# Gate products of a GRU by seven block products instead of eight, on one NeuronCore

## The chip, the cores and the metric

The kernel runs on one core of one Trainium2 chip. The metric is the device time of one execution in microseconds, taken on the slowest core, which here is the only one. Engines are named as in the profile: PE is the matrix engine (PEld its weight loads), DVE the vector engine, ACT the scalar engine, POOL the GpSimd engine, SP the queue that issues transfers.

## The reference

The input is 128 graphs of 128 nodes with 256 features, all float32, and an integer adjacency matrix for each graph. Four layers follow each other, and after each the result is added to its input and normalised over the features:

```python
# layer 0, three steps with shared GRU weights
for i in range(3):
    m = h @ weight[i]
    aggr = A.T @ m                       # A = (adj != 0)
    gi = aggr @ w_ih.T + b_ih ; gh = h @ w_hh.T + b_hh
    r = sigmoid(i_r + h_r) ; z = sigmoid(i_z + h_z) ; n = tanh(i_n + r * h_n)
    h = (1 - z) * n + z * h
x = layernorm(x + h)
# layers 1 to 3, each with its own W and a
Wh = x @ W.T ; e = leaky(Wh @ a1 [:, None] + Wh @ a2 [None, :]) masked by adj
x = layernorm(x + softmax(e) @ Wh)
```

## The kernel before

The 128 graphs are worked on in 32 groups of four (`G = 4`), so that a group's nodes fill 512 columns (`GN`). Features lie on partitions in two chunks of 128 (`KC = 2`). The function `gru` records layer 0 of a group, `gat` records layers 1 to 3 of it. Nothing is issued while they record: each operation goes to a `Plan` with the engines that may run it, a price in nanoseconds for each, the tiles it reads and writes, and the group's number as its priority. `Plan.order` then walks through time with these prices, gives every engine that is free the ready operation of the lowest group number for which slots are free, and returns one list. The engines' instruction streams follow that list, and each engine works its own stream strictly in order. So the order is fixed before the kernel runs, by the written prices.

Before the groups, three weight products `wc` (the message weight folded into the input weight, L488) and the score vectors `wa` (L496) are made.

A GRU step of a group goes like this. L317 multiplies the transposed state by the adjacency matrix into a `bank` tile of PSUM, and it is copied out as `agg` (L253 on ACT or L255 on DVE). The gates are the products of L328, in `gate` tiles of PSUM: for each of the two output chunks `c`, the accumulators `phn` (2 products with the state `hT`), `pr` (2 with `hT`, 2 with `agg`), `pin` (2 with `agg`) and `pz` (4), each product a 128x128 weight block against 512 columns. That is 24 products in a step and 2304 in the kernel. Then L343 (ACT, `q`), L347 (ACT, `tr`), L351 and L354 (DVE, `q` and `s`), L356 (ACT, `n`), L359 (ACT, `tz`), L362 (POOL, `d = hT - n`), L364 and L366 (DVE, `d` and the new `hT`) follow. L378 transposes the new state back for the next step.

A graph-attention layer begins when the layer norm of the one before (L278 and L280 on DVE, L282 and L284 on POOL, L287 on DVE) has given `xn`. Eight DVE operations at L400 (`fx`) form two scores for each of the four graphs, L409 on PE spreads them, L414 to L425 on DVE, L418 and L429 on ACT make the softmax, L436 transposes it, L452 and L463 on PE apply it and the weights (L463 has 128x256 products), and L469 on DVE scales and adds. While one group is in `gat`, the next is in `gru`; the list interleaves them.

## Time and profile before

| What | Value |
|---|---|
| median of 3 runs (lowest, highest) | 2953.62 us (2953.50, 2954.26) |
| the profiled execution, its time and its span | 2953.93 us, 2952.1 us |
| PE busy, matmul records | 2900.2 us, 11080 |
| DVE, ACT, POOL busy | 1729.7, 1079.8, 432.7 us |
| mean granted PE clock | 0.992 |
| one group in the steady part (2769.98 to 2859.55) | 89.57 us: PE 89.41, DVE 52.67, ACT 33.49, POOL 13.46 |

The profile counts two records for one float32 product (2304 products of L328 stand as two groups of 2304 records), so a product's price is that of two records. A record's mean duration includes the way through the array, which overlaps the next record; what a product costs PE is the distance between starts, and that is read from the timeline.

### The profile page before, as it was taken

Reading aid. Unit: us, or ns where it says so; the run is one execution under the profiler, and the core shown is the slowest. Engines: PE = TensorE matmul, PEld = TensorE weight load, DVE = VectorE, ACT = ScalarE, POOL = GpSimd, SP = SyncE. Lnnn points to the kernel's source line nnn. Section 1 sums busy time; section 2 is a strip of 40 time slices with the busy share of each in tenths; the row PEclk is TensorE's granted clock in tenths of the full one; section 3 lists DMA queues with packets and bytes.
Section 4 is the critical chain, followed back from the end, with each engine's and each line's share of the span. In section 5 each row is a group of like instructions: output and inputs, shape, how many; then the busy total and the mean of one; then the engine's idle time right before and its main releaser. Section 6 shows DMA issues by size and latency. Waiting matters only on the chain.

```text
span 2952.1 us, 31887 instructions
## 1 busy us (share of the span) xinstructions
PE 2900.2 (98%) x11080; PEld 1713.8 (58%) x11080; DVE 1729.7 (59%) x5639; ACT 1079.8 (37%) x2446; POOL 432.7 (15%) x454
## 2 busy tenths in 40 slices
PE   8999999999999999999999999999999999999994
PEld 4555565555555556555555655555655565565553
DVE  2566565556665655665665655566656556656654
ACT  2333333333343333333333334333433333333331
POOL 0111111111111111111111111111111111111110
PEclk9999999999999999999999999999999999999996
DMA  2000000000000000000000000000000000000000
GB/s 89 11 18 18 11 8 18 18 18 18 12 8 18 18 19 11 18 8 19 18 18 11 8 18 18 18 19 11 8 18 19 19 11 18 8 15 8 8 8 8
DMA packets 52001, 47.93 MB, mean 16 GB/s; under 512 B 2048, under 2 KB 51200, under 8 KB 51840
## 3 DMA queue, kind: packets, MB, share of 16 engines
q1 hardware_dynamic: 50688, 41.95, 4.5%
q10 hardware_dynamic: 1152, 3.94, 0.4%
q8 instruction: 87, 1.43, 0.2%
q14 instruction: 74, 0.61, 0.1%
HBM read 29.11 MB, written 16.78 MB: 16 GB/s over the span
## 4 chain that ended last, share of the span: by engine, by line
PE 88%; DVE 9%; POOL 2%; issue 0%; DMA 0%; ACT 0%; POOLq 0%; ACTq 0%; DVEq 0%
PE gate L328 59%; PE bank L463 9%; PE bank L452 6%; PE bank L317 6%; PE bank L378 3%; DVE fx L400 3%; DVE y L469 2%; POOL rstd L284 2%; DVE xn L287 2%; PE bank L436 2%; DVE st L278 2%; PE bank L409 1%; PE bank L268 1%; DVE mv L280 1%; POOL ve L282 1%; PE gate L488 1%
## 5 line engine op out<-in xcount | busy, mean ns | idle before, releaser
L328 PE MATMUL gate<-hT,whh 128*128 128x512 f32 x2304 | 1082.8, 593 | 0.0
L328 PE MATMUL gate<-agg,wc 128*128 128x512 f32 x2304 | 1072.0, 592 | 0.0
L328 PEld LDWEIGHTS gate<-agg,wc 128*128 128x128 f32 x2304 | 423.3, 190 | 447.7 <-issue 446.1
L328 PEld LDWEIGHTS gate<-hT,whh 128*128 128x128 f32 x2304 | 415.0, 191 | 387.0 <-issue 378.0
L362 POOL TENSOR_TENSOR d<-hT,n 128x512 f32<-128x512 f32 x192 | 243.9, 1271 | 1667.4 <-ACT n L356 1667.4
L463 PE MATMUL bank<-gwT,aT 128*128 128x256 f32 x1536 | 350.5, 381 | 0.0
L463 PEld LDWEIGHTS bank<-gwT,aT 128*128 128x128 f32 x1536 | 293.4, 191 | 81.0 <-issue 37.1
L359 ACT ACTIVATE tz<-gate,brz 128x512 f32<-128x512 f32 x192 | 130.8, 681 | 457.5 <-PE gate L328 457.5
L469 DVE SCALAR_TENSOR_TENSOR y<-bank,rden,xn 128x256 f32<-128x256 f32 x384 | 164.9, 471 | 199.0 <-PE bank L463 199.0
L400 DVE SCALAR_TENSOR_TENSOR fx<-xn,wa 128x256 f32<-128x256 f32 x768 | 272.5, 419 | 0.0
L351 DVE SCALAR_TENSOR_TENSOR q<-tr,q 128x512 f32<-128x512 f32 x192 | 132.1, 688 | 231.3 <-ACT tr L347 231.3
L347 ACT ACTIVATE tr<-gate,brz 128x512 f32<-128x512 f32 x192 | 131.9, 687 | 366.1 <-PE gate L328 366.1
L287 DVE TENSOR_SCALAR xn<-y,mv,rstd 128x256 f32<-128x256 f32 x512 | 176.8, 409 | 143.3 <-POOL rstd L284 143.3
L356 ACT ACTIVATE n<-s,bin__95 128x512 f32<-128x512 f32 x192 | 138.1, 719 | 329.6 <-DVE s L354 329.6
L452 PEld LDWEIGHTS bank<-pT,xn 128*128 128x128 f32 x1536 | 191.2, 196 | 47.4 <-issue 37.1
L364 DVE SCALAR_TENSOR_TENSOR d<-tz,d 128x512 f32<-128x512 f32 x192 | 131.9, 687 | 136.2 <-ACT tz L359 117.7
L278 DVE BATCH_NORM_STATS2 st<-y 128x6 f32<-128x256 f32 x512 | 207.3, 405 | 1.1
L418 ACT ACTIVATE e<-e,f 128x128 f32<-128x128 f32 x384 | 125.6, 390 | 211.2 <-DVE top L414 211.2
L452 PE MATMUL bank<-pT,xn 128*128 128x128 f32 x1536 | 192.5, 280 | 2.0 <-ACT pT L253 2.0
L354 DVE TENSOR_TENSOR s<-gate,q 128x512 f32<-128x512 f32 x192 | 132.4, 690 | 85.3 <-PE gate L328 75.4
L253 ACT COPY agg<-bank 128x512 f32<-128x512 f32 x161 | 94.2, 585 | 215.2 <-PE bank L317 215.2
L343 ACT ACTIVATE q<-gate,bhn 128x512 f32<-128x512 f32 x192 | 130.9, 682 | 113.6 <-PE gate L328 113.6
(55 smaller groups left out, 2239.0 us busy)
## 6 DMA issues: line engine op xcount, KB each, us to landing
xs<-in_x_dram SPq DMA_DIRECT2D x32, 512.0 KB, 3.9
out_dram<-xn SPq DMA_DIRECT2D x32, 512.0 KB, 2.9
adj<-in_adj_dram SPq DMA_DIRECT2D x32, 256.0 KB, 2.8
wih<-in_w_ihT_dram ACTq DMA_DIRECT2D x1, 768.0 KB, 5.3
gw<-in_gnn_wT_dram ACTq DMA_DIRECT2D x1, 768.0 KB, 7.8
whh<-in_w_hhT_dram ACTq DMA_DIRECT2D x1, 768.0 KB, 9.5
gwT<-in_gat_wT_dram ACTq DMA_DIRECT2D x1, 768.0 KB, 5.1
gatw<-in_gat_w_dram ACTq DMA_DIRECT2D x1, 768.0 KB, 6.3
```

The source lines that it names most:

```text
L278: plan.op({"DVE": 350}, lambda e, b=b, st=st: nc.vector.bn_stats(T(st), T(y)[:, b, :]), reads=[(y, b)], writes=[st], prio=prio)
L287: plan.op({"DVE": 345}, lambda e, b=b: nc.vector.tensor_scalar(T(dst)[:, b, :], T(y)[:, b, :], T(mv)[:, b, 0:1], T(rstd)[:, b:b + 1], op0= ...
L317: nc.tensor.matmul(T(b_)[:, b * P:(b + 1) * P], src, T(am)[:, b, :], start=True, stop=True)
L328: plan.op({"PE": 860}, lambda e, w=w, m=m, k=k, j=j: nc.tensor.matmul(T(dst), w(k), T(m), start=(j == 0), stop=(j == len(todo) - 1)), read ...
L351: plan.op({"DVE": 720}, lambda e, q=q, tr=tr: nc.vector.scalar_tensor_tensor(T(q), T(tr), 1.0, T(q), op0=ALU.add, op1=ALU.mult), reads=[tr ...
L354: plan.op({"DVE": 720}, lambda e, s=s, q=q, pin=pin: nc.vector.tensor_add(T(s), T(pin), T(q)), reads=[pin, q], writes=[s], prio=prio)
L356: plan.op({"ACT": 640}, lambda e, n=n, s=s, c=c: nc.scalar.activation(T(n), T(s), AF.Tanh, bias=bin_[:, c:c + 1]), reads=[s], writes=[n], ...
L362: plan.op({"POOL": 1266}, lambda e, d=d, n=n, c=c, hT=hT: nc.gpsimd.tensor_tensor(T(d), T(hT[c]), T(n), ALU.subtract), reads=[hT[c], n], w ...
L400: plan.op({"DVE": 345}, lambda e, b=b, h=h, l=l, f=f, fx=fx, xc=xc: nc.vector.scalar_tensor_tensor(T(fx), T(xc)[:, b, :], 1.0, wa[:, l, h, ...
L452: nc.tensor.matmul(T(b_)[:, b * P:(b + 1) * P], T(xc)[:, b, c * P:(c + 1) * P], T(pT)[:, b, :], start=True, stop=True)
L463: nc.tensor.matmul(T(b_)[:, (b - b0) * D:(b - b0 + 1) * D], T(aT[k])[:, b * P:(b + 1) * P], gwT[:, l, k, :], start=(k == 0), stop=(k == KC ...
L469: nc.vector.scalar_tensor_tensor(T(y)[:, b, :], T(b_)[:, (b - b0) * D:(b - b0 + 1) * D], T(rden)[:, b:b + 1], T(xc)[:, b, :], op0=ALU.mult ...
```

## The change

The gate products are made by a form of Strassen's algorithm (Winograd's). The 256x256 weight of each gate is taken as 2x2 blocks of 128x128, the 256x512 moving matrix as 2x2 blocks of 128x256, and the four blocks of the output come from seven block products in place of eight. The weights' sums (`block_sums`) are made once, at the beginning. The moving matrices' sums are made in each step, for `hT` and for `agg`, by four POOL subtractions of 128x256 each (`sums`, L374 of the changed program). In `strassen` the two gates r and z go together through three `gate` banks, and the two halves of n likewise; a bank is copied out on ACT (`kept`: L462, or L466 and L469) between products that go on accumulating in it, and DVE adds a kept part to a bank (`add`, L409 of the changed program). A product is now 128x128 by 128x256, 42 in a step (L404 of the changed program).

Beside that, SBUF tiles lose their own pools: there are a few sizes of slots (`k2`, `k4` and others), shared by all that fit, and the plan hands out the slot numbers, keeping some free for the oldest group (`own`). At most four groups may be in `gru` at a time (`gru`, 4). Group 0 makes the weights as part of the plan. The residual `x` is loaded a second time at the end of `gru`, and the mask `no` is made in place of `am`.

```diff
+    pools = {"gru": 4, "xs": 2, "adj": 2, "am": 4, "k2": 26, "k4": 18, "fx": 2, "f": 3, "mv": 4, "st": 6, "v": 16,
+             "gate": 5, "bank": 3}
+    own = {"k2": 8, "k4": 5, "gate": 2, "v": 5}
+    floats = {"gru": 0, "k4": 1024, "xs": 1024, "fx": 256, "f": 8, "mv": 8, "st": 6, "v": 4}
...
-    GATES, BANKS = 5, 3
-    pools = {"xs": 3, "adj": 2, "am": 2, "no": 3, "some": 3, "hT": 6, "agg": 4, "h2": 4, "q": 2, "tr": 2,
-             "s": 2, "n": 2, "tz": 2, "d": 2, "y": 2, "xn": 4, "f": 2, "fx": 2, "aT": 4, "e": 2, "p": 2, "pT": 2,
-             "mv": 4, "st": 4, "ve": 4, "rstd": 4, "top": 4, "nmax": 4, "den": 4, "rden": 4}
-    plan = Plan({**pools, "gate": GATES, "bank": BANKS})
...
+    def block_sums(dst, a, keys, prio):
+
+        d = T(dst)
+        todo = [(A11, lambda e: copy(e, d[:, A11], a(0, 0)), [], EVICT2),
+                (A12, lambda e: copy(e, d[:, A12], a(0, 1)), [], EVICT2),
+                (S1, lambda e: nc.vector.tensor_add(d[:, S1], a(1, 0), a(1, 1)), [], {"DVE": 600}),
+                (S2, lambda e: nc.vector.tensor_sub(d[:, S2], d[:, S1], a(0, 0)), [S1], {"DVE": 600}),
+                (S3, lambda e: nc.vector.tensor_sub(d[:, S3], a(0, 0), a(1, 0)), [], {"DVE": 600}),
+                (S4, lambda e: nc.vector.tensor_sub(d[:, S4], a(0, 1), d[:, S2]), [S2], {"DVE": 600}),
+                (N22, lambda e: nc.scalar.mul(d[:, N22], a(1, 1), -1.0), [], {"ACT": 500})]
+        for m, fn, more, engines in todo:
+            plan.op(engines, fn, reads=keys + [(dst, j) for j in more], writes=[(dst, m)], prio=prio)
...
+    def sums(ms, prio):
+
+        t = Buf("k4", 4, H)
+        first, second = (lambda: T(ms[0])[:, 0:H]), (lambda: T(ms[0])[:, H:GN])
+        third, fourth = (lambda: T(ms[1])[:, 0:H]), (lambda: T(ms[1])[:, H:GN])
+        part = lambda j: lambda: T(t)[:, j, :]
+        for j, (a, b, reads) in enumerate((
+                (second, first, [ms[0]]), (fourth, part(0), [ms[1], (t, 0)]), (fourth, second, ms),
+                (part(1), third, [ms[1], (t, 1)]))):
+            plan.op({"POOL": 700}, lambda e, j=j, a=a, b=b: nc.gpsimd.tensor_tensor(
+                T(t)[:, j, :], a(), b(), ALU.subtract), reads=reads, writes=[(t, j)], prio=prio)
+        return t
+
+    def moving(m, ms):
+
+        half = {A11: (0, 0), A12: (1, 0), S4: (1, 1)}
+        if m in half:
+            c, j = half[m]
+            return ms[0][c], lambda: T(ms[0][c])[:, j * H:(j + 1) * H]
+        j = {S1: 0, S2: 1, S3: 2, N22: 3}[m]
+        return (ms[1], j), lambda: T(ms[1])[:, j, :]
+
+    def strassen(gates, kept, prio):
+
+        bx, by, bz = Buf("gate", GN), Buf("gate", GN), Buf("gate", GN)
+        o0, o1 = Buf("k4", 2, GN), Buf("k4", 2, GN)
+        p1, u2, p5 = Buf("k2", GN), Buf("k2", GN), Buf("k2", GN)
+
+        def product(dst, m, first):
+            todo = [(j, gt, w, ms) for j, (gt, sides) in enumerate(gates) for w, ms in sides]
+            keys = {moving(m, ms)[0]: 0 for _, _, _, ms in todo}
+            keys.update({(w, m): 0 for _, _, w, _ in todo})
+            if first:
+                keys.update({(ms[1], 3): 0 for _, _, _, ms in todo})
+
+            def fn(e):
+                for n, (j, gt, w, ms) in enumerate(todo):
+                    nc.tensor.matmul(T(dst)[:, j * H:(j + 1) * H], T(w)[:, m, gt, :], moving(m, ms)[1](),
+                                     start=first and n == 0, stop=n == len(todo) - 1, skip_group_check=True)
+            plan.op({"PE": 432 * len(todo)}, fn, reads=list(keys), writes=[dst], prio=prio)
+
+        def add(b_, part, o, j):
+            plan.op({"DVE": 720}, lambda e: nc.vector.tensor_add(
+                T(o)[:, :, j * H:(j + 1) * H], T(b_).rearrange("p (g n) -> p g n", g=2),
+                T(part).rearrange("p (g n) -> p g n", g=2)),
+                reads=[b_, (part, 0), (part, 1)], writes=[(o, j)], prio=prio)
+
+        product(bx, A11, True)
+        kept(p1, bx, 0)
+        product(bz, S1, True)
+        kept(p5, bz, 1)
+        product(bx, S2, False)
+        kept(u2, bx, 0)
+        product(bz, S4, False)
+        add(bz, u2, o0, 1)
+        product(bx, S3, False)
+        add(bx, p5, o1, 1)
+        product(by, A12, True)
+        add(by, p1, o0, 0)
+        product(bx, N22, False)
+        return o0, o1, bx
...
-            def gate(dst, terms):
-
-                todo = [(w, m, k) for w, ms in terms for k, m in enumerate(ms)]
-                for j, (w, m, k) in enumerate(todo):
-                    plan.op({"PE": 860}, lambda e, w=w, m=m, k=k, j=j: nc.tensor.matmul(
-                        T(dst), w(k), T(m), start=(j == 0), stop=(j == len(todo) - 1)),
-                        reads=[m], writes=[dst], prio=prio)
-
-            def W(gt, c):
-                return lambda k: whh[:, k, gt * D + c * P:gt * D + (c + 1) * P]
-
-            def C(gt, c):
-                return lambda k, i=i: wc[:, i, k, gt * D + c * P:gt * D + (c + 1) * P]
-
+            h_in, a_in = (whs, (hT, sums(hT, prio))), (wcs[i], (agg, sums(agg, prio)))
+
+            def whole(dst, src, c):
+                plan.op({"ACT": 560}, lambda e: nc.scalar.copy(T(dst), T(src)),
+                        reads=[src], writes=[(dst, 0), (dst, 1)], prio=prio)
+
+            def halves(dst, src, c):
+                plan.op({"ACT": 370}, lambda e: nc.scalar.activation(
+                    T(dst)[:, 0:H], T(src)[:, 0:H], AF.Identity, bias=bhn[:, c:c + 1]),
+                    reads=[src], writes=[(dst, 0)], prio=prio)
+                plan.op({"ACT": 370}, lambda e: nc.scalar.copy(T(dst)[:, H:GN], T(src)[:, H:GN]),
+                        reads=[src], writes=[(dst, 1)], prio=prio)
+
+            rz = strassen([(0, (h_in, a_in)), (1, (h_in, a_in))], whole, prio)
+            nn = strassen([(2, (h_in,)), (2, (a_in,))], halves, prio)
+            hT2 = []
             for c in range(KC):
...
+
+                o, v, d = rz[c], nn[c], Buf("k2", GN)
+
+                def tanh(gt, n0, n1, src, o=o, c=c):
+                    nc.scalar.activation(T(o)[:, gt, n0:n1], src(), AF.Tanh,
+                                         bias=brz[:, gt * KC + c:gt * KC + c + 1], scale=0.5)
+                for gt in range(2):
+                    if c == 0:
+                        plan.op({"ACT": 640}, lambda e, gt=gt, o=o, tanh=tanh: tanh(gt, 0, GN, lambda: T(o)[:, gt, :]),
+                                reads=[(o, 0), (o, 1)], writes=[(o, 2 + gt)], prio=prio)
+                    else:
+                        plan.op({"ACT": 420}, lambda e, gt=gt, tanh=tanh, rz=rz: tanh(
+                            gt, 0, H, lambda: T(rz[2])[:, gt * H:(gt + 1) * H]),
+                            reads=[rz[2]], writes=[(o, 4 + gt)], prio=prio)
+                        plan.op({"ACT": 400}, lambda e, gt=gt, o=o, tanh=tanh: tanh(gt, H, GN, lambda: T(o)[:, gt, H:GN]),
+                                reads=[(o, 1), (o, 4 + gt)], writes=[(o, 2 + gt)], prio=prio)
+                if c == 1:
+                    plan.op({"ACT": 370}, lambda e, v=v, nn=nn: nc.scalar.activation(
+                        T(v)[:, 0, 0:H], T(nn[2])[:, 0:H], AF.Identity, bias=bhn[:, 1:2]),
+                        reads=[nn[2]], writes=[(v, 0)], prio=prio)
+                plan.op({"DVE": 720}, lambda e, o=o, v=v: nc.vector.scalar_tensor_tensor(
+                    T(v)[:, 0, :], T(o)[:, 0, :], 1.0, T(v)[:, 0, :], op0=ALU.add, op1=ALU.mult),
+                    reads=[(o, 2), (v, 0), (v, 1)], writes=[(v, 2)], prio=prio)
+                if c == 0:
+                    plan.op({"DVE": 720}, lambda e, v=v: nc.vector.tensor_add(T(v)[:, 0, :], T(v)[:, 1, :], T(v)[:, 0, :]),
+                            reads=[(v, 2)], writes=[(v, 3)], prio=prio)
+                else:
+                    plan.op({"DVE": 430}, lambda e, v=v, nn=nn: nc.vector.tensor_add(
+                        T(v)[:, 0, 0:H], T(nn[2])[:, H:GN], T(v)[:, 0, 0:H]),
+                        reads=[(v, 2), nn[2]], writes=[(v, 3)], prio=prio)
+                    plan.op({"DVE": 430}, lambda e, v=v: nc.vector.tensor_add(
+                        T(v)[:, 0, H:GN], T(v)[:, 1, H:GN], T(v)[:, 0, H:GN]),
+                        reads=[(v, 2)], writes=[(v, 4)], prio=prio)
+                plan.op({"ACT": 640}, lambda e, v=v, c=c: nc.scalar.activation(
+                    T(v)[:, 0, :], T(v)[:, 0, :], AF.Tanh, bias=bin_[:, c:c + 1]),
+                    reads=[(v, 3), (v, 4)], writes=[(v, 5)], prio=prio)
+
+                plan.op({"POOL": 1266}, lambda e, d=d, v=v, h_=hT[c]: nc.gpsimd.tensor_tensor(
+                    T(d), T(h_), T(v)[:, 0, :], ALU.subtract), reads=[hT[c], (v, 5)], writes=[d], prio=prio)
+                plan.op({"DVE": 720}, lambda e, d=d, o=o: nc.vector.scalar_tensor_tensor(
+                    T(d), T(o)[:, 1, :], 1.0, T(d), op0=ALU.add, op1=ALU.mult), reads=[(o, 3), d], writes=[d], prio=prio)
+                plan.op({"DVE": 720}, lambda e, d=d, v=v: nc.vector.scalar_tensor_tensor(
+                    T(d), T(d), 0.5, T(v)[:, 0, :], op0=ALU.mult, op1=ALU.add), reads=[d, (v, 5)], writes=[d], prio=prio)
+                hT2.append(d)
             if last:
-                y = sb("y", G, D)
-                h2 = None
+                y = Buf("k4", G, D)
+                plan.op({"SP": 60}, lambda e: nc.sync.dma_start(T(y), x_g), reads=[agg[0]], writes=[y], prio=prio)
+                plan.op({"DVE": 720}, lambda e: nc.vector.tensor_reduce(T(some), T(am), AX.X, ALU.max),
+                        reads=[am], writes=[some], prio=prio)
+                plan.op({"DVE": 417}, lambda e: nc.vector.tensor_scalar(
+                    T(am), T(am), 0.0, FAR, op0=ALU.is_equal, op1=ALU.mult), reads=[am], writes=[am], prio=prio)
...
```

## The prediction

> **What bounds the kernel now.** I read the table of engines first, then the chain that ended last, then one stretch of the timeline, then the waits.
>
> The table of engines and the chain by line:
>
> ```profile
> PE 2900.2 (98%) x11080; PEld 1713.8 (58%) x11080; DVE 1729.7 (59%) x5639; ACT 1079.8 (37%) x2446; POOL 432.7 (15%) x454
> ...
> PE gate L328 59%; PE bank L463 9%; PE bank L452 6%; PE bank L317 6%; PE bank L378 3%; DVE fx L400 3%; DVE y L469 2%; POOL rstd L284 2%; DVE xn L287 2%; PE bank L436 2%; DVE st L278 2%; PE bank L409 1%; PE bank L268 1%; DVE mv L280 1%; POOL ve L282 1%; PE gate L488 1%
> ```
>
> PE is the bound, and the gate products L328 carry most of the chain. The DVE and POOL entries are stretches where the chain goes through an attention layer's scores and normalisation while PE is busy with other groups, and the last group's layers, with which nothing is left to interleave. Busy time may flatter a pipelined engine, so the price of a product comes from starts in PE's timeline:
>
> ```profile
> 1508.46 1.95 PE L452 MATMUL bank<-pT,xn 128*128 128x128 f32 x16
> 1510.24 0.60 PE L378 MATMUL bank<-ident,hT 128*128 128x128 f32 x4
> 1510.68 1.02 PE L328 MATMUL gate<-hT,whh 128*128 128x512 f32 x2
> 1511.54 3.62 PE L463 MATMUL bank<-gwT,aT 128*128 128x256 f32 x16
> 1515.00 1.05 PE L317 MATMUL bank<-am,h 128*128 128x128 f32 x8
> 1515.89 1.02 PE L328 MATMUL gate<-hT,whh 128*128 128x512 f32 x2
> 1516.75 3.60 PE L328 MATMUL gate<-agg,wc 128*128 128x512 f32 x8
> 1520.18 1.88 PE L328 MATMUL gate<-hT,whh 128*128 128x512 f32 x4
> ```
>
> Each start follows the one before at the price of the work, without a hole. Eight 512-column records take 3.43 us; the chain in order of time has 42 of them in 18.03 us, so 0.4293 a record and **0.8586 us a product**. L463 is the shape to come: 256 columns, fresh weights for each product, 16 records from 1511.54 to 1515.00, so 0.2163 a record and **0.4325 us a product**. Its weight loads (191 ns) hide under 216 ns.
>
> **The PE term.** Removed: 2304 products x 0.8586 = 1978.2 us. Added: 42 in each of 96 steps, 4032 x 0.4325 = 1743.8 us. Gain **234.4 us**, 7.33 us a group, from 89.57 to 82.2. The other PE work of the program's order is unchanged in number.
>
> The Trainium skill (Perfetto Trace Analysis, Matmuls) says larger matmuls are more efficient than smaller ones, which speaks against halving the width. The rows show how much: two halves cost 0.865 against 0.8586, 0.7%, and that is inside the sum already.
>
> **What the other engines get, per group.** DVE: busy 52.67 us in the window of one group (2769.98 to 2859.55), 53.67 in the one before; I take 53.7. New are 18 additions from PSUM (L409) at 0.69 by row L354, 3 additions in SBUF at 0.69 by L351, 6 half ones at 0.42 by L400; gone are 6 of L354: 12.4 + 2.1 + 2.5 - 4.1 = 12.9, so 66.6 of 82.2 us. ACT: 33.5; gone are q, tr and tz (6 x 0.68 = 4.1 a step, without n); new 3 copies at 0.585, 6 halves and one more at about 0.4, tanh 2 x 0.69 and 4 x 0.45, 7.7 a step: 44.5. POOL: 13.5, and 24 subtractions of 128x256. No row has that shape. Half of L362 (1.271 at 512 columns) is 0.64; a line from L282's least 0.224 (4 columns) gives 0.75. I take 0.70: 16.8 more, **30.3 us, 37% of the time**. None passes PE. The second load of x (32 x 512 KB on SP, 3.9 us to landing) lies beside a transfer share of 0.05.
>
> **Covers.** An operation off PE is free only if PE has other work, in its fixed order, while it runs. I summed the cadences of the PE work that stands in the changed program's order between a product and the one that needs its result, for groups 8 to 27.
>
> Between products on one bank: 1.30 us at least for n, 1.73 for r and z. Needed: 0.20 from the last record's start to the reader's (1510.68 to L255 at 1510.88), two half copies (L490's 0.37 and one with a bias, together 0.79), 0.06 for the signal: 1.05. Covered by a quarter of a microsecond; DVE and ACT must come on time.
>
> Between two steps of a group: 15.3 us at least, other boundaries 21 to 43. Needed: 0.20, identity 0.45, L351 0.69, two half additions 0.78, tanh 0.72, L362 1.27, L364 and L366 1.41, transposes 0.64, copy 0.69, L317 1.10, copy 0.58, four sums 2.80, ten signals 0.60: 11.9. Cost taken as nothing; with the 3.4 us gone, POOL's and DVE's waits there (about 1.3 us a step, a third of a chance for each of some ten operations to meet the other engine for 0.4) would cost 125 us.
>
> From an attention layer's last product to the next layer's L409: 7.8 us, against 7.7 in the order of before. There before has no slack:
>
> ```profile
> PEld bank L409 <- DVE fx L400: 51.0, 163, 0.5
> ...
> PE bank L409 <- DVE fx L400: 23.8, 42, 6.3
> ```
>
> PE meets these eight DVE operations as they end; any lateness of `fx` becomes a PE wait.
>
> **Where lateness comes from.** DVE and POOL block each other. Around one `d` of POOL:
>
> ```profile
> 1548.66 0.16 DVE L421 SCALAR_TENSOR_TENSOR top<-top,f 128x4 f32<-128x4 f32 x1
> 1548.86 1.12 DVE L425 SCALAR_TENSOR_TENSOR nmax<-top 128x4 f32<-128x4 f32 x1
> ```
>
> ```profile
> 1548.68 1.28 POOL L362 TENSOR_TENSOR d<-hT,n 128x512 f32<-128x512 f32 x1 [6.47 <-ACT n L356]
> ```
>
> The row of L425 in the view by source line:
>
> ```profile
> L425 DVE SCALAR_TENSOR_TENSOR nmax<-top x96: 161/163/1131, 116.2 to 2932.0; 128x4 f32<-128x4 f32 x96
> ```
>
> An operation of 0.16 us lasts until POOL is done, in 31 of 96 cases. The other way round, L282 (0.23) takes 0.59 beside L364. Additions with a PSUM input (L469) do not stretch beside POOL. No `fx` meets POOL before; it will. A chain of eight takes 2.76 us (starts 0.345 apart), meets 37% x 2.76 = 1.02 us of POOL work, 96 times: 98 us if all of it falls on `fx`, nothing if all falls on POOL. Who issues first wins, and the sums have 3.4 us of cover, so I take half: **49 us**.
>
> The Trainium skill (SBUF — State Buffer, Who interferes with whom) makes this a rule: a DVE instruction with two SBUF inputs and a GpSimd instruction that reads SBUF exclude each other, and the loser blocks. The rows agree (1.12 for 0.16). By it every such operation counts, not `fx` alone; the slower rival below is what the sum would be then.
>
> **Head and tail.** The weights' 36 wide products stay; before the first gate product there are now copies and block sums (some five in a row at 0.4 to 0.6, less the overlap): 5 us, between 0 and 15. At the end the way from the last product to the state is identity, L351, two halves, tanh, POOL, two DVE, 5.3 us, against L359, L364, L366 at 2.1; with a step boundary near its cover I take 5 us, between 3 and 15. Together **10 us**.
>
> **Sum.** 2953.9 (the profiled execution; the median is 0.3 less) - 234.4 + 49 + 10 = **2778 us**.
>
> **The rivals.**
> (1) *Everything is covered*: POOL's work meets DVE only where slack is; then the lock's term is 0: 2953.9 - 234.4 + 0 to 35 = 2720 to 2755. For it: the order of before, with the same covers, leaves 89.41 of 89.57 us busy although L425 is late 31 times. Against it: POOL has more than twice the work.
> (2) *Slower: the lock reaches PE from every chain.* DVE's time with two SBUF inputs is 24 x 0.345 + 18 x 0.69 + 3 x 0.69 + 3 x 0.42 = 24 us a group; 37% of it meets POOL, 8.9 us. If all of that stops PE: 2953.9 - 234.4 + 285 + 10 = 3014. It decides from 7.0 us a group on (224 / 32), four fifths of the meeting. For it: PE works in order, and inside a step the cover is 0.25 us. Against it: half should fall on POOL, and a PE that waits once gives all later operations that slack.
> (3) *The change does not do what it says*, because narrow products cost more than half. L463 excludes it by the same shape and fresh weights.
>
> **Chances.** Forecast (PE the bound, part of the lock on its path, 2755 to 2948) 0.55; rival 1 0.27; rival 2 0.16; a gain that is just eaten 0.02. The bounds together: least 2712 (gain alone, and 7 us of the small PE waits of before gone); above, 98 for `fx`, half of the 125 at the steps and 25 for the ends give 2953.9 - 234.4 + 98 + 62 + 25 = 2905. Left out are rival 2, the eaten gain and 0.02 of the forecast: 0.20. Faster by over 0.2% (6 us, about what a measurement of this kernel can tell from no change) 0.82, within it 0.02, slower 0.16.
>
> **What would show it.** Right: L404 at 0.2163 us a record between starts; a group's period near 84 us; PE busy near 96%; PE's waits at the transposes of `f` grown by 1 to 2 us a group; `fx` no longer 411 to 425 ns throughout but with some at 0.8 to 1.1; subtractions of 0.70 that stretch to 1.0 beside DVE. Rival 1: a period of 82.2. Rival 2: a period above 89.57, PE under 91% busy, waits of PE for L409 and the ACT copies inside a step. The prediction would be wrong at its root if L404's records stood further apart than 0.22 us with no wait between them.

## The result and the profile after

The changed kernel takes **3037.8 us** (median of four runs, 3037.5 to 3039.1) against 2953.6 for the kernel before (four runs, 2953.3 to 2954.3). The ratio is 1.0286, 95% interval 1.0268 to 1.0303: 2.9% slower, where 2778 us was forecast, with a range up to 2905. The profiled execution has a span of 3035.8 us and a mean granted clock of 0.963; before it was 0.992.

The table of engines of the changed kernel, and its chain by line:

```profile
PE 2790.6 (92%) x14536; PEld 2425.0 (80%) x14536; DVE 2338.3 (77%) x6340; ACT 1357.3 (45%) x3406; POOL 1074.1 (35%) x1222
...
PE 52%; DVE 32%; POOL 10%; ACT 3%; issue 3%; DMA 1%; DVEq 0%; POOLq 0%; ACTq 0%
PE gate L404 36%; DVE fx L559 8%; DVE k L360 6%; PE bank L622 5%; POOL k L374 5%; PE bank L611 4%; DVE k L628 3%; DVE st L351 3%; POOL v L357 3%; PE bank L454 3%; DVE k L517 2%; DVE k L496 2%; DVE k L515 2%; DVE k L409 2%; POOL k L513 2%
```

The first line gives a balance. The 234.4 us of the forecast go into it as given; what supports them is the spacing of the products below, and the run below with narrow sums and 600 ns hand-overs, in which PE is busy for 2678.0 us. PE's idle time, span less busy, went from 51.9 us to 245.2: 193.3 more. Its busy time should have fallen by the 234.4 us of the forecast, to 2665.8; it is 2790.6, so its records got 124.8 us longer than planned. 193.3 + 124.8 - 234.4 = 83.7, the whole difference of the spans. The saving was there, and waits and slow records took it back and more. In the chain, PE fell to half, and DVE and POOL carry 42% of it. L559 is the score product `fx`, L360 the normalisation, L374 the sums, L513 the state's subtraction `d`, L515 and L517 the state updates after it, L568 the transposes of `f`, L534 those of the state.

The balance also says by how much the forecast missed. It allowed 49 + 10 = 59 us over the saving. Over the saving are 193.3 + 124.8 = 318.1: PE's waits for `fx` grew by 92.2 us (23.8 before, 116.0 now), those at the state's transposes by 60.4 (2.1 before, 62.5 now), its other idle time by 40.7, and its records by 124.8.

The products themselves cost what was forecast. PE's timeline, from a stretch without waits (start, length, engine, line, and after the names the number of records):

```profile
1502.09 0.59 PE L404 MATMUL gate<-k,wcs 128*128 128x256 f32 x2
...
1503.40 0.60 PE L404 MATMUL gate<-k,whs 128*128 128x256 f32 x2
1503.83 0.59 PE L404 MATMUL gate<-k,wcs 128*128 128x256 f32 x2
```

Two records in 0.43 us, 0.216 each. PE's largest waits (total, times, longest):

```profile
PE bank L568 <- DVE fx L559: 116.0, 133, 6.2
PE bank L534 <- DVE k L517: 62.5, 49, 4.9
...
PE gate L404 <- DVE k L409: 8.9, 15, 2.3
```

Nearly all of it stands at transposes. Inside a step, where the cover was a quarter of a microsecond, PE loses 9 us; and PE never waits for a sum itself: no line of this view has L404 behind L374. The groups of the score product and the normalisation (busy time, mean ns of one):

```profile
L559 DVE SCALAR_TENSOR_TENSOR fx<-k,wa 128x256 f32<-128x256 f32 x768 | 340.4, 507 | 0.0
...
L360 DVE TENSOR_SCALAR k<-k,mv,v 128x256 f32<-128x256 f32 x512 | 256.2, 563 | 100.5 <-POOL v L357 100.5
```

Before, these means were 419 and 409. The excess, 0.088 x 768 and 0.154 x 512, is 68 and 79 us; added over all of DVE's lines (without its reads of accumulators), the time above the shortest tenth of each line's operations is 314 us, where it was 54 before. In the trace after, every one of the 121 `fx` and 166 normalisations that took over 1.3 times the median lies beside a sum or a `d` of POOL; in the trace before, not one of the 768 and 512 ran beside POOL work for more than 50 ns. Two pieces of the timeline show how it reaches PE. First the state's transposes, on DVE, POOL and PE:

```profile
1507.41 2.75 DVE L360 TENSOR_SCALAR k<-k,mv,v 128x256 f32<-128x256 f32 x4 [0.38 <-POOL v L357]
1510.08 0.68 DVE L537 TENSOR_TENSOR k<-bank,k 128x512 f32<-128x512 f32 x1
1510.68 0.67 DVE L409 TENSOR_TENSOR k<-gate,k 128x512 f32<-128x512 f32 x1
1511.28 0.70 DVE L515 SCALAR_TENSOR_TENSOR k<-k,k 128x512 f32<-128x512 f32 x1
1512.08 0.69 DVE L517 SCALAR_TENSOR_TENSOR k<-k,k 128x512 f32<-128x512 f32 x1
```

```profile
1507.87 1.41 POOL L513 TENSOR_TENSOR k<-k,k 128x512 f32<-128x512 f32 x1 [0.49 <-ACT k L509]
1509.24 2.19 POOL L374 TENSOR_TENSOR k<-k,k 128x256 f32<-128x256 f32 x3
```

```profile
1510.77 0.59 PE L404 MATMUL gate<-k,wcs 128*128 128x256 f32 x2
1512.83 0.66 PE L534 MATMUL bank<-ident,k 128*128 128x128 f32 x4 [1.47 <-DVE k L517]
```

`d` is done at 1509.28. DVE can't take it up, since its order has four normalisations, an addition to a bank and a gate addition first, and the normalisations lasted 2.75 us beside POOL, where four at 0.409 would be under 1.7. PE waits 1.47 us at the end of that queue, and products that need nothing of this stand behind L534.

Second the score products, on DVE and on POOL: three of them last as long as POOL's sums run, and the fourth, after the sums, takes 0.41 us again.

```profile
1569.94 0.94 DVE L559 SCALAR_TENSOR_TENSOR fx<-k,wa 128x256 f32<-128x256 f32 x1
...
1570.81 0.93 DVE L559 SCALAR_TENSOR_TENSOR fx<-k,wa 128x256 f32<-128x256 f32 x1
...
1571.67 0.93 DVE L559 SCALAR_TENSOR_TENSOR fx<-k,wa 128x256 f32<-128x256 f32 x1
...
1572.54 0.41 DVE L559 SCALAR_TENSOR_TENSOR fx<-k,wa 128x256 f32<-128x256 f32 x1
```

```profile
1569.83 2.50 POOL L374 TENSOR_TENSOR k<-k,k 128x256 f32<-128x256 f32 x3
```

On PE these are two waits, and after them its clock falls:

```profile
1571.03 0.29 PE L568 MATMUL bank<-ident,f 128*128 128x128 f32 x1 [1.22 <-DVE fx L559]
1572.67 0.32 PE L568 MATMUL bank<-ident,f 128*128 128x128 f32 x1 [1.34 <-DVE fx L559]
...
1574.32 1.06 PE L404 MATMUL gate<-k,whs 128*128 128x256 f32 x2
1575.18 1.06 PE L404 MATMUL gate<-k,wcs 128*128 128x256 f32 x2
...
1576.78 0.60 PE L404 MATMUL gate<-k,wcs 128*128 128x256 f32 x2
```

And the view by windows over those products (window, its length, busy time of PE, PEld, DVE, ACT, POOL, then the granted clock):

```profile
1500.00:1570.00 70.00, 65.46 (x349) 56.58 (x347) 60.54 (x159) 31.55 (x78) 32.85 (x39) 0.98 0.07 23
...
1574.30:1576.50 2.20, 2.20 (x7) 1.75 (x7) 2.13 (x14) 1.31 (x5) 0.00 (x0) 0.50 0.00 0
```

Products start 0.86 us a pair apart instead of 0.43, at half the clock, and nothing waits. There are 39 such stretches, of 3.4 or 6.8 us mostly, 229 us in all; before there were four, 51 us, in the last group alone. Of the 39, 29 begin within 5 us after two or three waits that are each shorter than 2 us, and 8 after a longer wait. Sixteen waits of 1.4 to 2.0 us that stood alone, the one of 1.47 us at L534 above among them, had no halved clock in the 4 us after them. The waits do not settle it: three of 0.89, 1.4 and 0.37 us in a row came before a halved clock eight times, and once, at 545 us, none followed them.

### The profile page after: what moved, and what is told of

Same layout as the page of the kernel before. It is cut to its first block, busy times and chain, and to the rows that moved or that the text cites. A ratio compares the mean times of both kernels' runs of the same rounds, so it can differ in the third digit from the quotient of the medians.

```text
span 3035.8 us, 42078 instructions
## 1 busy us (share of the span) xinstructions
PE 2790.6 (92%) x14536; PEld 2425.0 (80%) x14536; DVE 2338.3 (77%) x6340; ACT 1357.3 (45%) x3406; POOL 1074.1 (35%) x1222
## 4 chain that ended last, share of the span: by engine, by line
PE 52%; DVE 32%; POOL 10%; ACT 3%; issue 3%; DMA 1%; DVEq 0%; POOLq 0%; ACTq 0%
PE gate L404 36%; DVE fx L559 8%; DVE k L360 6%; PE bank L622 5%; POOL k L374 5%; PE bank L611 4%; DVE k L628 3%; DVE st L351 3%; POOL v L357 3%; PE bank L454 3%; DVE k L517 2%; DVE k L496 2%; DVE k L515 2%; DVE k L409 2%; POOL k L513 2%
## 5 line engine op out<-in xcount | busy, mean ns | idle before, releaser
L404 PE MATMUL gate<-k,whs 128*128 128x256 f32 x4032 | 1228.6, 387 | 10.0 <-DVE k L409 8.9
L404 PE MATMUL gate<-k,wcs 128*128 128x256 f32 x4032 | 1218.9, 384 | 0.0
L404 PEld LDWEIGHTS gate<-k,wcs 128*128 128x128 f32 x4032 | 780.8, 194 | 110.8
L404 PEld LDWEIGHTS gate<-k,whs 128*128 128x128 f32 x4032 | 746.2, 195 | 101.9 <-DVE k L409 15.3
L374 POOL TENSOR_TENSOR k<-k,k 128x256 f32<-128x256 f32 x576 | 482.7, 862 | 176.0 <-DVE k L517 105.0
L409 DVE TENSOR_TENSOR k<-gate,k 128x512 f32<-128x512 f32 x576 | 386.2, 684 | 189.1 <-PE gate L404 173.6
L513 POOL TENSOR_TENSOR k<-k,k 128x512 f32<-128x512 f32 x192 | 256.2, 1337 | 482.8 <-ACT k L509 482.5
L261 ACT COPY k<-bank 128x512 f32<-128x512 f32 (+1 forms) x513 | 293.2, 582 | 234.9 <-PE bank L454 78.0
L622 PE MATMUL bank<-gwT,k 128*128 128x256 f32 x1536 | 350.6, 381 | 0.2
L559 DVE SCALAR_TENSOR_TENSOR fx<-k,wa 128x256 f32<-128x256 f32 x768 | 340.4, 507 | 0.0
L360 DVE TENSOR_SCALAR k<-k,mv,v 128x256 f32<-128x256 f32 x512 | 256.2, 563 | 100.5 <-POOL v L357 100.5
L622 PEld LDWEIGHTS bank<-gwT,k 128*128 128x128 f32 x1536 | 291.2, 191 | 41.5 <-ACT k L261 2.7
L374 POOL TENSOR_TENSOR k<-k 128x256 f32<-128x256 f32 x192 | 157.3, 820 | 382.4 <-ACT k L261 310.2
L462 ACT COPY k<-gate 128x512 f32<-128x512 f32 x288 | 168.1, 584 | 265.3 <-PE gate L404 263.4
```

What stands on the lines that cost most here:

```text
L261: nc.scalar.copy(dst, src)
L360: plan.op({"DVE": 345}, lambda e, b=b: nc.vector.tensor_scalar(T(dst)[:, b, :], T(y)[:, b, :], T(mv)[:, b, 0:1], T(rstd)[:, b:b + 1], op0= ...
L374: plan.op({"POOL": 700}, lambda e, j=j, a=a, b=b: nc.gpsimd.tensor_tensor(T(t)[:, j, :], a(), b(), ALU.subtract), reads=reads, writes=[(t, ...
L404: nc.tensor.matmul(T(dst)[:, j * H:(j + 1) * H], T(w)[:, m, gt, :], moving(m, ms)[1](), start=first and n == 0, stop=n == len(todo) - 1, s ...
L409: plan.op({"DVE": 720}, lambda e: nc.vector.tensor_add(T(o)[:, :, j * H:(j + 1) * H], T(b_).rearrange("p (g n) -> p g n", g=2), T(part).re ...
L513: plan.op({"POOL": 1266}, lambda e, d=d, v=v, h_=hT[c]: nc.gpsimd.tensor_tensor(T(d), T(h_), T(v)[:, 0, :], ALU.subtract), reads=[hT[c], ( ...
```

## The experiments

Two theories stood at the outset. *Lock*: DVE and POOL exclude each other, and the sums' POOL time reaches PE. *Order*: the changed program's fixed order leaves no room where an operation comes late, so that PE stops, and its clock then falls. The expectations call them theory A and theory B; a theory C, that PE waits for the sums themselves, finds nothing in PE's waits above. Each experiment is a single run, except where it says otherwise; repeated times of one kernel here lie within 6 us of each other (2833.7 to 2839.0 for the order that was repeated).

**The lock: four kernels that change the sums.**

*Narrow sums* keep the order, with 8 of the 256 columns subtracted:

```diff
-                T(t)[:, j, :], a(), b(), ALU.subtract), reads=reads, writes=[(t, j)], prio=prio)
+                T(t)[:, j, 0:8], a()[:, 0:8], b()[:, 0:8], ALU.subtract), reads=reads, writes=[(t, j)], prio=prio)
```

> The changed kernel in its own order, but each POOL subtraction of the sums covers 8 of its 256 columns (the output then lacks the rest of the sums; the slots are filled once at the beginning, some 5 us). POOL's work falls from 1074 us to about 600. Theory A (DVE and POOL exclude each other, and the lateness stops PE): fx at 0.42 throughout, PE waits from 236 us to under 80, 2720 to 2790 us. Theory B (the order has too little cover, whatever POOL does): waits stay, above 2950 us. Theory C (the sums are simply later than their price of 0.70 us, and PE waits for them): like A here.

Measured: 2822.0 us, 216 less than the changed kernel; `fx` 419 ns in the mean, the normalisation 464. So this change in POOL's work alone decides between slower and faster than before. It takes away three things at once: POOL's reading, its writing, and the time until a sum is there. PE's two largest waits in it (its lines stand three further down, so L537 is L534 and L571 is L568):

```profile
PE bank L537 <- DVE k L520: 34.4, 35, 4.9
PE bank L571 <- DVE fx L562: 27.9, 36, 6.2
```

In the same order the wait for `fx` is nearly back at the 23.8 us of before, so nearly all of its growth goes with the sums. At the state's transposes 34.4 of 62.5 us stay: there the order is short of cover even with POOL out of the way.

*Fills in place of the sums* keep POOL's time (0.74 us each), write 768 columns each where a sum writes 256, and read nothing:

```diff
-            plan.op({"POOL": 700}, lambda e, j=j, a=a, b=b: nc.gpsimd.tensor_tensor(
-                T(t)[:, j, :], a(), b(), ALU.subtract), reads=reads, ...
+            plan.op({"POOL": 700}, lambda e, j=j, a=a, b=b: nc.gpsimd.memset(
+                T(t).rearrange("p a b -> p (a b)")[:, 256 * (j == 3):768 + 256 * (j == 3)], 0.5), reads=reads, ...
```

> The changed kernel in its own order, but each subtraction of the sums is a POOL fill of 768 columns, which takes about as long (0.6 to 0.8 us) and reads nothing (the sums are then constants). Theory A, if the exclusion is about reading SBUF: as without the sums, 2720 to 2850 us, with fx not stretched by the fills. If it is about any use of SBUF: about 3000 us. Theory C (POOL's time itself is late): 2950 to 3040 us. Theory B: 2950 to 3040 us.

Measured: 2922.2 us. Its two groups:

```profile
L360 DVE TENSOR_SCALAR k<-k,mv,v 128x256 f32<-128x256 f32 x512 | 300.4, 648 | 100.0 <-POOL v L357 100.0
...
L559 DVE SCALAR_TENSOR_TENSOR fx<-k,wa 128x256 f32<-128x256 f32 x768 | 277.4, 423 | 0.0
```

The score product with its two SBUF inputs is free again (423 ns), and the normalisation with one input is stopped more than ever (648 ns, the longest 3.38 us). All 201 normalisations over 1.3 times the median lie beside a fill, so writing alone stops L360. 319 `fx` lie beside fills alone and none of them takes over 420 ns, so `fx` is stopped by POOL's reading, not by its writing. The time, 2922, lies between what the theories expected (2850 at most, or 2950 at least). How the 216 us divide, 116 with the reading and 100 without, is only a rough guide: the fills write three times as much, and, reading nothing, they also wait for nothing. POOL idles 23 us before the fills, where it idled 555 before the sums.

*The sums on DVE* (`"POOL": 700` becomes `"DVE": 360`, and the operation is VectorE's):

> The changed kernel with the sums on DVE at a price of 360 ns (new order). DVE's work rises by 24 x 0.35 = 8.4 us a group, to about 75 of 82. Theory A: POOL as short as before, little exclusion, 2750 to 2900 us. Theory B: above 2950 us, since DVE is fuller and covers no longer. Theory C: 2750 to 2900 us.

Measured: 2957.1 us, still not under the kernel before. `fx` takes 419 ns, L360 441, so the lock is nearly gone; yet PE idles 199.8 us and waits 65.2 for `fx` and 30.3 for L517. The lock can't be all of it. That a late DVE, 80% busy, does here what a stopped one does is argued: this is also another order.

*The kernel before with the same eight subtractions a step*, read by nobody:

```diff
+            extra(hT, prio)
+            extra(agg, prio)
             hT2 = [sb("hT", GN) for c in range(KC)]
```

> The kernel before, with the same eight POOL subtractions a step added, whose results nobody reads. Theory A: fx and the normalisation stretch as in the changed kernel, PE waits at the transposes of f; with the share that the changed kernel shows (about 7 us a group more waiting) 3050 to 3250 us. Theories B and C: nobody waits for these results, 2950 to 2970 us.

Measured: 2988.6 us, 34 more than the kernel before, between the two expectations. L287, its normalisation, goes from 409 to 503 ns and `fx` from 419 to 438, and DVE's busy time for the same operations from 1729.7 to 1873.9 us. So POOL's work meets DVE here too, and 144 us of it on DVE lengthen the run by 34, where in the changed kernel 260 go with 216. That its order and its eight wide products a gate leave the room is argued.

**The order: the same operations, other hand-overs in the planner.** A hand-over is the passing of a result from one engine to another. The planner takes a result as there for another engine 120 ns after its operation ends (250 after PE's). With 600:

```diff
-                when = max([t + (0 if e2 == e else self.LATENCY.get(e2, 120)) for e2, t in o.at.items()], default=0)
+                when = max([t + (0 if e2 == e else self.LATENCY.get(e2, 600)) for e2, t in o.at.items()], default=0)
```

> Same operations and engines as the changed kernel; the planner is told that a result reaches another engine 600 ns after its operation ends instead of 120 (PE's 250 stay), so that the fixed order leaves about 0.5 us of other work at each hand-over to or between DVE, ACT and POOL. Theory A (the meeting of DVE and POOL reaches PE whatever the order): DVE's stretch is near 285 us again and the time within 30 us of 3038. Theory B (an order without cover turns each lateness into a PE wait, and the waits into a slower clock): the stretch is as large but PE's gaps fall from 236 us to under 130, the time to 2860 to 2940.

Measured: 2833.7 us, 204 less than the changed kernel and 120 less than the one before (the planner also moves 40 copies, which either engine may do, from DVE to ACT). Engines and PE's waits:

```profile
PE 2708.3 (96%) x14536; PEld 2384.9 (84%) x14536; DVE 2286.8 (81%) x6300; ACT 1382.2 (49%) x3446; POOL 1087.9 (38%) x1222
```

```profile
PE bank L568 <- DVE fx L559: 63.2, 85, 7.9
...
PE bank L534 <- DVE k L517: 10.7, 10, 2.6
```

PE idles 123.6 us instead of 245.2, and its records are 42.5 us over plan instead of 124.8. DVE's time above its shortest operations is 298 us by the same sum, against 314. The lateness is there; far less of it stops PE. The gain is larger than the order theory expected.

Is that room, or a lucky order? A list scheduler answers any edit with another order. Two controls, at 120 ns and at 600, change only the planned price of a sum from 700 to 690 ns:

> The changed kernel with the planner's price of a sum at 690 ns instead of 700: an order as tight as before, but another one. If the run with 600 ns hand-overs was only a luckier order, this one can land anywhere between 2830 and 3040. If room at the hand-overs is what counts (theory B), it stays within 50 us of 3038, with PE's gaps above 190 us.

Measured: 3010.0 us, with PE idle for 247.8: what was expected if room counts.

> Hand-overs planned at 600 ns as in the run that gave 2834, and the price of a sum 690 ns instead of 700: a second order with the same room. At 120 ns this edit moved the time by 28 us. If room sets the time, 2820 to 2920 (the run with 700 ns gave 2918); if 600 was luck alone, as likely near 2970 or above.

Measured: 2938.2 us, more than room alone was expected to give. Two more points, at 400 and 700 ns:

> The changed kernel with a planned hand-over of 400 ns, between 120 (3038) and 600 (2834). If room at the hand-overs is the cause, the time falls with it: 2880 to 2960. If 600 was a lucky order, there is no relation, and any value from 2830 to 3040 is as likely.

Measured: 2967.5 us, just above what was expected.

> The changed kernel with a planned hand-over of 700 ns, beyond the 600 that gave 2834. Room as the cause: 2800 to 2870, since most lateness is one stretch of 0.4 to 0.7 us and more room has little left to cover. A lucky order at 600: above 2900 here.

Measured: 2918.0 us, where room was to give 2870 at most and a lucky order at 600 above 2900: by its own expectation this run speaks for luck. So both: orders without room gave 3038 and 3010, with 600 or 700 ns they gave 2834, 2938 and 2918; and two orders with the same room differ by 104 us. PE's waits tell the parts from each other. Those for L517 at the state's transposes fall with the room: 62.5 and 60.0 us at 120 ns, 35.3 at 400, 10.7 and 15.1 at 600, 10.1 at 700. Those at `fx` do not follow it:

```profile
PE bank L568 <- DVE fx L559: 103.1, 105, 7.9
PE bank L534 <- DVE k L517: 15.1, 21, 2.6
```

This is the second order at 600 ns: L534 as good, L568 40 us worse, with `fx` at 511 ns and L360 at 538 where the first had 474 and 513. How often these two meet POOL is what the order happens to give.

The issues of the output show where the 104 us lie. After the first ten or so groups these orders run in cycles. The view by windows from one issue of the output to a later one, first the changed kernel, one cycle of 6 groups:

```profile
1142.63:1692.21 549.58, 515.54 (x2714) 449.96 (x2713) 439.35 (x1186) 251.38 (x633) 203.21 (x229) 0.97 0.07 21
```

The first order at 600 ns, 19 groups:

```profile
1030.36:2612.38 1582.02, 1567.11 (x8578) 1389.39 (x8577) 1350.55 (x3726) 811.15 (x2031) 643.79 (x716) 1.00 0.07 22
```

The second order at 600 ns, one cycle of 10 groups:

```profile
1123.10:2003.88 880.78, 842.92 (x4521) 745.83 (x4520) 721.21 (x1970) 423.85 (x1061) 342.90 (x381) 0.98 0.07 22
```

That is 91.6, 83.3 and 88.1 us a group, with the granted clock at 0.97, 1.00 and 0.98; the kernel before has 89.6 us. In the first order at 600 ns every group of this stretch takes the same time, PE is 99% busy and the clock does not fall: the period near 84 us that was forecast does exist, in an order in which PE seldom waits. In the other two some groups of each cycle take over 95 us. The gap of 4.8 us a group between the two orders at 600 ns makes up, over some twenty groups, nearly all of the 104 us.

Room at one hand-over alone (`lag=1000` at L559's operation, the rest at 120):

> The changed kernel with one hand-over alone given room: the planner takes each score product's result (fx, L559) as there 1 us later, so that PE has about 1 us more work before the transposes of f (L568), at which it lost 149 us. All other hand-overs stay at 120 ns. Theory B: the loss at L568 falls to under 80 us and the time by 60 to 120 us, to 2920 to 2980, with L534 (the state's transposes) left as the largest wait. Theory A: the meeting of DVE and POOL delays fx by what it delays it, PE only waits elsewhere: 3010 or more.

Measured: 2997.2 us, 41 less, where theory B expected 60 to 120. The wait at L568 falls from 116.0 to 106.1 us only. That asking for one result earlier doesn't help while what stands ahead of it in DVE's queue comes late is argued, since the rest of the order changed with it (the wait at L534 fell to 38.9 us).

Both cures at once complete a square:

> Both cures at once: sums of 8 of 256 columns (outputs are then not the reference's) in the order with 600 ns hand-overs. With the run of narrow sums in the tight order (2822) and that of full sums in the roomy order (2834) it completes a square. If each cure takes away what the other would (lateness that needs both a meeting and a missing cover): 2780 to 2815. If they add up, 3038 - 216 - 204 would be 2620, below PE's own work; the floor by PE's work and the ends is some 2680 to 2700.

Measured: 2759.4 us, a little under what was expected.

| time, us | order with 120 ns | with 600 ns | room is worth |
|---|---|---|---|
| sums of 256 columns | 3037.8 | 2833.7 | 204 |
| sums of 8 columns | 2822.0 | 2759.4 | 63 |
| POOL's work costs | 216 | 74 | |

Each cure is worth three times as much where the other is missing: the changed kernel loses its time where lateness and missing room come together. The left column is one order, the right another, and orders with equal room differed by up to 104 us, so the 204 and the 74 hold for these two orders.

The kernel before with 600 ns:

> The kernel before with the 600 ns hand-over in its planner. Its PE had gaps of 43 us only, and its eight wide products a gate leave room in any order. Theory B: little to gain, 2925 to 2960. If the long hand-over is worth as much by itself as in the changed kernel (some planner fault that both share): below 2900, and then the change is worth less than the 120 us by which it beats the kernel before with that hand-over.

Measured: 2941.3 us, 12 less. Its order had little to gain, so the change with a good order is worth 108 us, not 120.

**True prices, and normalisation on ACT.** Told the durations of the changed kernel's trace (sums 860 ns, `d` 1340, L360 480, `fx` 432, the state updates 840) and 400 ns:

> Same operations; the planner is told what they took in the changed kernel's trace (sums on POOL 860 ns instead of 700, the subtraction of the state 1340 instead of 1266, normalisation 480 and score products 432 instead of 345, the three state updates 840 instead of 720), and a hand-over of 400 ns instead of 120. Theory A: no order helps, 3000 to 3040. Theory B: 2840 to 2920, PE's gaps under 130 us.

Measured: 2882.1 us, within what theory B expected, though PE still idles 154.8 us. It is 85 less than 400 ns without the prices, within the scatter just seen. Normalisation on ACT, without and with the true prices, both at 120 ns (`shift` is one small DVE operation a norm, left out here):

```diff
-            plan.op({"DVE": 345}, lambda e, b=b: nc.vector.tensor_scalar(
-                T(dst)[:, b, :], T(y)[:, b, :], T(mv)[:, b, 0:1], T(rstd)[:, b:b + 1], ...
+            plan.op({"ACT": 370}, lambda e, b=b: nc.scalar.activation(
+                T(dst)[:, b, :], T(y)[:, b, :], AF.Identity, bias=T(shift)[:, b:b + 1], scale=T(rstd)[:, b:b + 1]),
```

> The normalisation (L360, one-input operations that stretched by 80 us) goes to ACT as a scaled identity with a bias, which costs DVE one small operation a norm; prices and hand-over as in the changed kernel. DVE's busy time falls by about 280 us to some 2060, ACT's grows by 190 to 1550. Theory A: the part of the stretch in the normalisation stood ahead of the score products on the way to PE's transposes, so the time falls by 60 to 120 us to 2920 to 2980; the score products still stretch by some 70 us. Theory B: the order still has no cover, and the time falls by less than 50 us, to 2990 or more.

Measured: 2964.9 us, 73 less: what theory A expected (60 to 120), and more than theory B did (under 50).

> Normalisation on ACT as in the run before, and the planner is told the measured prices of the sums, the state's subtraction, the score products and the state updates; the hand-over stays at 120 ns. If the order needs only true prices (a sharper form of theory B): 2840 to 2900, PE's gaps under 130 us. If lateness comes by chance and must be given room at each hand-over: above 2920, since mean prices leave none. Theory A: within 30 us of the run before.

Measured: 2962.4 us: mean prices alone give nothing more, as both theory A and lateness that comes by chance would have it. With room, the move to ACT did not add up:

> Three edits at once: normalisation on ACT, hand-overs planned at 300 ns, and each score product taken as there 2 us later. One hand-over given 1 us alone gained 41 us, normalisation on ACT alone 73. If room at the one place where most is lost plus a lighter DVE is enough: 2780 to 2830, under the 2834 of 600 ns everywhere. If lateness is carried along DVE's whole queue, so that room at a few places does not stop it: 2860 to 2930.

Measured: 2878.7 us.

> Normalisation on ACT and hand-overs planned at 600 ns. With little cover the move to ACT gained 73 us. If what is left of the lock in the roomy order (74 us by the narrow sums) is DVE's load and stretch, this takes part of it: 2780 to 2820. If the extra step from DVE through ACT back to DVE costs what it saves: 2830 or more.

Measured: 2914.9 us. Neither is faster than the plain 600 ns order: with the normalisation off DVE's queue, the score products met POOL more often (562 and 551 ns in the mean, where the plain order has 474). That this ate the gain is argued, not shown. The plain order was then run five times:

> The same kernel as the first run with 600 ns hand-overs, timed in five rounds against the kernel before. Its order is fixed, so its time should come again: 2825 to 2845, a ratio of 0.957 to 0.963. Luck in that single run would show as a median above 2850.

Measured: 2838.0 us (2835.0 to 2839.0), ratio 0.9608, interval 0.9595 to 0.9621. A version of the change that beats both kernels exists, with one number of the planner changed.

## Why the prediction was wrong

**PE's gain: right.** 0.2163 us a record was forecast, 0.216 measured. With narrow sums and room PE's busy time is 2678.0 us, 12 over the forecast's 2665.8, and in the first order at 600 ns a group takes 83.3 us, for a forecast near 84. ACT was forecast at 44.5 us a group and has 42.4 (1357.3 / 32), POOL at 30.3 and has 33.6, since its sums take 0.82 to 0.86 in the mean beside DVE, not 0.70. DVE has 73.1 for 66.6; its stretch, 260 us more than before, is 8.1 a group and covers the difference.

**The lock's term, 49 us: the size failed, at two choices.** "So I take half" supposed that half of each meeting falls on POOL, and that only `fx` counts. DVE's stretch grew by 260 us and POOL's, by the same sum, by 112, so some seven tenths fell on DVE. Its 8.1 us a group are nine tenths of the 8.9 that the slower rival had worked out as the full meeting, though not on the same operations. L360, left out for its single SBUF input, alone has 79 us of it; the trace before, in which no normalisation runs beside POOL for more than 50 ns, could not show that. In PE's waits for `fx` alone the term measured 92 us, and all that the sums' POOL work costs in this order, clock and all, is 216. The Trainium skill (SBUF — State Buffer, Who interferes with whom) bears on the second choice: a two-input operation collides with a GpSimd operation that reads and not with one that only writes, and `tensor_scalar` can collide through its two-port modes. The fills agree on both counts (423 and 648 ns). The prediction took only the first half of the rule into account.

**"Cost taken as nothing" at the step's end: the step that failed in kind.** 15.3 us of PE work against 11.9 needed was a sum over the path's own operations. It left out what stands between them in DVE's queue (at 1507.41 above, some 4 us of other work ahead of L515), and it ended at the first product of the next step, though PE is in order and stops already at L534. The prediction's price for the cover's loss, 125 us, was about as far off as the nothing it took: the wait at L534 is 62.5 us, before the clock, and 34.4 of it stay when the sums are narrow.

**No term for the clock.** 124.8 us of PE's records are over plan. By the clocks, (1 - 0.963) x 3035.8 less (1 - 0.992) x 2952.1, some 89 us of it can be the clock, an estimate; the rest I can't split, since ends of records are modelled. The Trainium skill (TensorE: Matmul & The Clock Gate, HAM oscillation) warns of PE gaps above some 3.4 us; here two of 1.2 and 1.3 us, close together, came before a halved clock, and single ones of up to 2.0 us had none after them.

**Rivals.** The slower one (3014) was 24 us off, and a group's period is above 89.57 us, as it said. That its number came so close is in part luck. Its 285 us for the lock compare with 216 that go with the sums' POOL work here, and the clock, for which it had no term, is in them. It was wrong about the place: it expected waits inside a step, at the gate additions and copies, and those are 10 us; and PE is 92% busy, not under 91. And it is not the lock alone: the same order with narrow sums still has 2822. The first rival (2720 to 2755) is close to what narrow sums give in an order with room, 2759. Of the 10 us for head and tail the trace shows less: the first gate product starts at 32.1 us, where it started at 34.1, and from the start of the last one to the end it is 78.7 us, where it was 75.1.

**What stays open**: which property of an order decides the cycle into which it falls, and with it how often `fx` and L360 meet POOL: some 100 us between two orders with equal room.

## What to carry to other kernels

Cover for a moved step is not PE work against the path's own operations: add what stands ahead of each of them in its engine's queue, and end the sum at the first instruction of the in-order engine that waits, even a small transpose. Work put on an idle POOL was paid for on DVE, seven tenths of it here; price it by everything on DVE that it can stop, the operations with one input too. Where a planner writes the order, give each hand-over room for the lateness that the trace shows, and try several orders before judging a change: here the order was worth 204 us, nearly as much as the 234 us of arithmetic saved. And look at the time of each group, not at the total alone: a cycle that is uneven from group to group shows an order with waits in it.

## What the hardware showed that was not expected

In the changed kernel the granted clock halved after waits of little more than a microsecond where two or three came within some 5 us, mostly for 3.4 or 6.8 us: 229 us of its span, 51 before. Sixteen single waits of 1.4 to 2.0 us left it whole there. POOL's writing alone, without reading, stops a one-input normalisation of 128x256 on DVE: 648 ns in the mean and 3.38 us at the longest, where it takes 409.
